# Value projection as seven block products, with context sums made in the load buffers

## The chip, the cores and the metric

The kernel runs on one core of one Trainium2 chip. Its time is the device time of one execution in microseconds (us), and the median of several executions is compared. Five engines work side by side, each through its own queue of instructions in order: TensorE (PE; the loading of its weights is shown apart as PEld), VectorE (DVE), ScalarE (ACT), GpSimd (POOL) and SyncE (SP, which here only issues transfers). Transfers between the chip's main memory and the on-chip memory run on 16 DMA engines.

## The reference

One layer of a perceiver: cross-attention of 64 queries to a context of 1024 rows for each of 16 batch items, then self-attention, then a quantised feed-forward part. The change touches the two projections of the context, `key @ Wk` and `value @ Wv`.

```python
def _L0_xattn_ref(query, key, value, Wq, Wk, Wv, Wo):   # key = value = ctx, 16 x 1024 x 1024
    q = (query @ Wq).reshape(b, sq, 32, 32).transpose(0, 2, 1, 3)
    k = (key @ Wk).reshape(b, sk, 8, 32).transpose(0, 2, 1, 3)      # Wk: 1024 x 256
    v = (value @ Wv).reshape(b, sk, 8, 32).transpose(0, 2, 1, 3)    # Wv: 1024 x 256
    k = jnp.repeat(k, 4, axis=1)
    v = jnp.repeat(v, 4, axis=1)
    scores = jnp.einsum('bhqd,bhkd->bhqk', q, k) * 32 ** -0.5
    probs = jax.nn.softmax(scores, axis=-1)
    out = jnp.einsum('bhqk,bhkd->bhqd', probs, v)
    return out.transpose(0, 2, 1, 3).reshape(b, sq, 1024) @ Wo

x = x + _L0_xattn_ref(_layernorm(x), ctx_4096, ctx_4096, Wq, Wk, Wv, Wo)
x = x + _L0_attn_ref(_layernorm(x), ...)
x = x + _L0_ffn_ref(_layernorm(x), ...)
```

All of this part is in 32-bit floats.

## The kernel before

The cross-attention is a loop over 32 units, n = 0 to 31. Unit n belongs to batch item b = n // 2 and to one half g of the eight key heads. Each unit has four slots, i = 0 to 3, and every engine's instructions stand in the order in which the loop writes them. In a slot of unit n TensorE computes scores of the unit that follows (`by_key`, L575, two tiles of 128 keys, into two pairs of PSUM banks that are used again in the next slot). ScalarE copies them to on-chip memory (L587) while VectorE keeps a running maximum (L591 in slot 0, L594 after it); the two take turns on the two pairs. After slot 3 `reduce` finds the maxima of the unit (L599 to L606), and `spread` sends them through main memory to all partitions. In slots 1 and 2 the current unit's exponentials are made, two per slot: VectorE subtracts the maxima (L618, 128 x 2048, both inputs in on-chip memory), ScalarE takes exp (L619), and GpSimd adds up the rows (`sums`, L625 for the first tile, L628 after it). TensorE's products with the values (L637), the sums over partitions (L647) and the quotients (L656, L661, L663, L666) follow in slots 2, 0 and 1.

Between these, TensorE takes steps from a list, `fillers`: the projection of the next batch item's context to keys and values. `fill(2)` stands early in a slot, a second `fill` late in it. The list of item b + 1 is made at the start of unit 2b and is used up by the end of unit 2b + 1. For items 2 to 15 (`fast`: 1 <= b < 15, that is n = 2 to 29) `project_fast` makes it.

There the keys are not computed as eight block products but as seven. The context of an item is seen as 2 x 2 blocks, quarter(b, h, i): h is the half of the 1024 rows, i the half of the 1024 features. The weights are 2 x 2 blocks too, i the half of the features and g the half of the 256 columns. The sums of context blocks are made by transfers: SP loads a quarter into a buffer, and GpSimd issues transfers that add further quarters to it in place. `chained` holds quarter(1,0) + quarter(1,1), then also + quarter(0,0), then also + quarter(0,1); `paired` holds quarter(1,0) + quarter(0,0). Sums of weight blocks are made once (`weight_sums`, L366 to L369). The seven products are called z5, p1, p2, z6, z7, z4 and p3; each is four matmul calls of 512 columns (L407), made in two steps of two calls, and each result is taken out of PSUM by ScalarE (a copy, L442) or VectorE (L445, L453, L458, L463), with one more operation on GpSimd (L446). p2 adds to the bank of p1, and p3 to that of z5. The values are computed plainly (L426): for each of eight tiles of 128 rows eight calls of 256 columns, in steps of four calls, copied by ScalarE (L434). A 32-bit matmul call is two weight loads and two matmul instructions in the trace.

The context itself is loaded in halves of 2 MB by SP (`load_context`) into two buffers that are used in turn (`stream`, at 64 and 80 KB of the arena), and the quarters of `chained` and `paired` (8 and 16 KB) are transferred again beside them. Three PSUM banks hold the projection's products. A tile of keys (`kT`) is read by the score matmuls: those of slots 2 and 3 of unit 2b + 1 read the second half of the rows of item b + 1, first half of the columns (k21), which z7 and z4 make.

In all units up to the end of the preparation of the feed-forward weights, `treat_piece` has ScalarE work on a piece of these weights in some slots (L522, L526, L530), with a load or a store on SP. In unit 8 `thresholds` reduces over them.

## Time and profile before

| | us |
|---|---|
| median of 3 runs | 1867.86 (1863.75 to 1868.98) |
| span of the profiled execution | 1863.3 |
| units 2 to 29, first score group of the first to the end of the last | 260.08 to 1261.90 |
| a pair of units in the middle (two score groups 0, 875.31 to 945.51) | 70.2 |

The page of the profile gives, for the whole execution, the granted clock of TensorE in 40 slices (tenths of full speed) and the busy shares of the other engines:

```
PE   8999999999899999999999999999999999899999
DVE  3011587777877887877887887877524257775554
ACT  1233656665566776776776776544101123664221
POOL 1000446655565576576566565566503424455520
PEclk9999999999999999999999999999999999899999
```

One slice is 46.6 us. The stage in question fills slices 6 to 27. Its costliest groups (line, engine, operation, output and input, count, busy us, mean ns of one, idle time before them and what ended it):

```
L628 POOL TENSOR_TENSOR arena<-arena 128x1024 f32<-128x1024 f32 x192 | 541.7, 2821 | 20.5 <-ACT arena L619 8.5
L426 PE MATMUL v<-arena 128*128 128x256 f32 x1792 | 405.2, 382 | 1.2 <-ACT arena L442 1.2
L618 DVE TENSOR_TENSOR arena<-arena 128x2048 f32<-128x2048 f32 x128 | 373.5, 2958 | 4.3 <-DMA arena<-tops 4.3
L407 PE MATMUL z<-arena 128*128 128x512 f32 x560 | 260.6, 608 | 11.3 <-ACT arena L442 5.3
L594 DVE TENSOR_TENSOR arena<-t,arena 128x512 f32<-128x512 f32 x384 | 258.9, 688 | 211.6 <-PE t L575 155.3
L587 ACT COPY arena<-t 128x1024 f32<-128x1024 f32 x256 | 254.8, 1009 | 209.1 <-PE t L575 118.0
```

Matmuls are pipelined, so the mean of one is longer than the distance between two.

### The profile page before, as it was taken

The numbers are of one execution on the slowest core, as the hardware profiler recorded it, in microseconds if no ns is written. First come the engines' busy times: TensorE is split into PE (matmuls) and PEld (weight loads), VectorE is DVE, ScalarE is ACT, GpSimd is POOL, SyncE is SP. The second block draws the span as 40 slices with busy tenths as digits, with TensorE's granted clock in tenths as the row PEclk, the third lists the DMA queues.
The fourth block names the chain that finished last, engine by engine and source line by source line (L and its number), as shares of the span: only waits on it lengthen the run. The fifth ranks groups of instructions, "written<-read, shape, count | busy, mean of one in ns | idle before, by whom it ended". The sixth has DMA issues, their size and how long they took to land.

```text
span 1863.3 us, 26374 instructions
## 1 busy us (share of the span) xinstructions
PE 1822.5 (98%) x10880; PEld 1080.9 (58%) x10880; DVE 1219.1 (65%) x1436; ACT 926.5 (50%) x988; POOL 885.8 (48%) x505
## 2 busy tenths in 40 slices
PE   8999999999899999999999999999999999899999
PEld 5445565565565665665665665664446454566654
DVE  3011587777877887887887887877524257775554
ACT  1233656665566776776776776544101123664221
POOL 1000446655565576576566566565503424455520
PEclk9999999999999999999999999999999999899999
DMA  9234578777687787886787787663120032243201
GB/s 346 69 106 139 187 223 271 224 231 237 188 262 196 253 254 191 263 254 195 254 252 201 251 254 202 198 186 153 36 75 19 1 77 62 51 130 109 75 29 51
DMA packets 64264, 314.65 MB, mean 169 GB/s; under 512 B 10192, under 2 KB 19344, under 8 KB 47376
## 3 DMA queue, kind: packets, MB, share of 16 engines
q1 hardware_dynamic: 52848, 242.99, 37.1%
q0 software_dynamic: 10144, 67.88, 17.2%
q10 hardware_dynamic: 1152, 2.10, 0.3%
q8 instruction: 85, 1.39, 0.3%
q14 instruction: 35, 0.29, 0.0%
HBM read 293.74 MB, written 19.20 MB: 168 GB/s over the span
## 4 chain that ended last, share of the span: by engine, by line
PE 66%; DVE 2%; POOL 2%; ACT 1%; DMA 1%; issue 1%; ACTq 0%; POOLq 0%; DVEq 0%
PE v L426 15%; PE z L407 10%; PE wo L250 6%; PE t L575 5%; PE q L250 5%; PE o L637 5%; PE d L1040 4%; PE p L407 4%; PE g L961 3%; PE gu L961 3%; PE v L740 1%; PE k L250 1%; POOL arena L628 1%; DMA arena<-in_ctxT 1%; PE o L647 1%
## 5 line engine op out<-in xcount | busy, mean ns | idle before, releaser
L628 POOL TENSOR_TENSOR arena<-arena 128x1024 f32<-128x1024 f32 x192 | 541.7, 2821 | 20.5 <-ACT arena L619 8.5
L426 PE MATMUL v<-arena 128*128 128x256 f32 x1792 | 405.2, 382 | 1.2 <-ACT arena L442 1.2
L594 DVE TENSOR_TENSOR arena<-t,arena 128x512 f32<-128x512 f32 x384 | 258.9, 688 | 211.6 <-PE t L575 155.3
L426 PEld LDWEIGHTS v<-arena 128*128 128x128 f32 x1792 | 336.8, 190 | 78.6 <-issue 29.5
L618 DVE TENSOR_TENSOR arena<-arena 128x2048 f32<-128x2048 f32 x128 | 373.5, 2958 | 4.3 <-DMA arena<-tops 4.3
L587 ACT COPY arena<-t 128x1024 f32<-128x1024 f32 x256 | 254.8, 1009 | 209.1 <-PE t L575 118.0
L619 ACT ACTIVATE arena<-arena 128x2048 f32<-128x2048 f32 x128 | 244.6, 1911 | 168.6 <-DVE arena L618 167.8
L625 POOL TENSOR_TENSOR arena<-arena 128x1024 f32<-128x1024 f32 x32 | 75.8, 2368 | 524.6 <-ACT arena L619 491.1
L407 PE MATMUL z<-arena 128*128 128x512 f32 x560 | 260.6, 608 | 11.3 <-ACT arena L442 5.3
L250 PE MATMUL q<-arena 128*128 128x512 f32 x512 | 224.6, 595 | 0.6 <-ACT arena L287 0.6
L407 PEld LDWEIGHTS z<-arena 128*128 128x128 f32 x560 | 103.2, 192 | 138.1 <-issue 117.5
L250 PEld LDWEIGHTS q<-arena 128*128 128x128 f32 x512 | 95.6, 190 | 116.4 <-issue 114.3
L575 PE MATMUL t<-arena 32*128 32x256 f32 x2048 | 146.6, 400 | 1.3 <-ACT arena L346 1.2
L961 PEld LDWEIGHTS <-arena 128*128 128x128 bf16 x1024 | 98.8, 98 | 64.7 <-issue 13.7
L591 DVE TENSOR_REDUCE arena<-t 128x512 f32<-128x1024 f32 x64 | 74.7, 1204 | 90.9 <-PE t L575 90.9
L575 PEld LDWEIGHTS t<-arena 32*128 32x128 f32 x2048 | 93.1, 184 | 66.6 <-issue 61.4
L637 PE MATMUL o<-arena 128*32 128x256 f32 x2048 | 123.8, 382 | 0.0
L250 PE MATMUL wo<-arena 128*128 128x512 f32 x256 | 112.3, 595 | 0.3 <-ACT arena L287 0.3
L407 PE MATMUL p<-arena 128*128 128x512 f32 x224 | 108.2, 605 | 0.0
L637 PEld LDWEIGHTS o<-arena 128*32 128x32 f32 x2048 | 60.0, 109 | 68.7 <-issue 32.0
L722 POOL TENSOR_TENSOR arena<-arena 128x512 f32<-128x512 f32 x20 | 33.5, 1673 | 133.6 <-DVE arena L720 133.6
L961 PE MATMUL gu<-arena 128*128 128x344 fp8e4 x544 | 85.3, 314 | 9.6 <-ACT arena L969 6.5
(146 smaller groups left out, 1974.6 us busy)
## 6 DMA issues: line engine op xcount, KB each, us to landing
arena<-in_ctxT SPq DMA_DIRECT2D x31, 2048.0 KB, 11.4
arena<-in_ctxT POOLq DMA_DIRECT2D x56, 1024.0 KB, 11.4
arena<-in_ctxT SPq DMA_DIRECT2D x28, 1024.0 KB, 12.1
arena<-tops SPq DMA_DIRECT2D x48, 512.0 KB, 4.9
arena<-in_wg SPq DMA_DIRECT2D x32, 688.0 KB, 4.5
arena<-in_wu SPq DMA_DIRECT2D x32, 688.0 KB, 6.2
arena<-in_wd SPq DMA_DIRECT2D x32, 688.0 KB, 9.2
arena<-ternary POOLq DMA_DIRECT2D x26, 344.0 KB, 3.8
```

What stands on the lines that cost most here:

```text
L250: nc.tensor.matmul(made[0], lhsT=lhsT(k), rhs=rhs(k), start=(k == 0), stop=(k == KC - 1))
L407: nc.tensor.matmul(held[n], lhsT=weights[:, k, :], rhs=what()[:, k, :], start=(first and k == 0), stop=(k == 3), skip_group_check=not first,)
L426: nc.tensor.matmul(held[n][:, bass.ts(at, KVD)], lhsT=ctx_halves[b, h][:, k, bass.ts(kts[at], P)], rhs=wkvs[:, k, KVD:], start=(k == 0), s ...
L575: nc.tensor.matmul(ws[jj // 2][:, jj % 2, a, :], lhsT=self.kT[rows, self.g, bass.ts(i * 2 + a, P)], rhs=two_tiles[self.b // 2 % 2][rows, s ...
L587: nc.scalar.copy(pt[:, 2 * mine : 2 * mine + 2], ws[mine])
L594: nc.vector.tensor_tensor(m, w[:, :, a], m, ALU.max)
L618: nc.vector.tensor_tensor(pt, pt, by.to_broadcast([P, 4, 2, 256]), ALU.subtract)
L619: nc.scalar.activation(pt, pt, AF.Exp)
L625: nc.gpsimd.tensor_tensor(acc, pt[:, :, 0], pt[:, :, 1], ALU.add)
L628: nc.gpsimd.tensor_tensor(acc, acc, pt[:, :, a], ALU.add)
L637: nc.tensor.matmul(self.po[bass.ts(jj, HD), 0:256], lhsT=self.v[:, kt, bass.ts(self.g * 4 + jj, HD)], rhs=self.pts[i][:, jj, a, :], start= ...
L961: nc.tensor.matmul(ps[:, :CW], lhsT=xqT[t][:, k, :], rhs=wbs[n][i][:, k, :], start=(k == 0), stop=(k == KC - 1),)
```

## The change

The values of items 2 to 15 are now made of seven block products too. `product` has a `kind`: 0 for keys, as before, and 1 for values, where the context block is the stationary operand and the weight block (128 columns) the moving one: 16 calls of 128 columns for each product, in two steps of eight. The list of steps goes from 30 to 28, and the second `fill` of slot 2 takes one step instead of two. Both kinds read the same four buffers: the chain, `paired`, `second_in` and `last_in`. The context is no longer loaded in halves: p1 reads `paired` while it still holds one quarter, before the other is added to it, and p2 and z4 read quarters of their own. There are two chain buffers, used in turn by items, at 64 and 8 KB; `second_in` and `last_in` lie at 72 and 80 KB, and the second set of weight sums at 88 KB, in the room of the two stream buffers. Each kind has its results taken out by three ScalarE copies, four VectorE operations and two GpSimd operations; p3 no longer adds to z5's bank, and GpSimd adds z5's block instead. The transfers and some sums stand elsewhere in the loop.

```diff
-    chained, paired = (place(kb, [4, 512]) for kb in (8, 16))
-    w_sums = place(24, [4, 4, P])
+    chains = [place(kb, [4, 512]) for kb in (64, 8)]
+    paired, second_in, last_in = (place(kb, [4, 512]) for kb in (16, 72, 80))
+    w_sums = [place(kb, [4, 4, P]) for kb in (24, 88)]
...
+    def load_quarter(dst, *of):
+        nc.sync.dma_start(dst, quarter(*of))
+
+    def add_quarter(dst, *of):
+        nc.gpsimd.dma_start(dst, quarter(*of), accum_op=ALU.add)
+
+    def chain_of(b):
+        return chains[b % 2]
...
+                else:
+                    for kt in (2 * i, 2 * i + 1):
+                        for k in range(4):
+                            nc.tensor.matmul(
+                                ps[:, bass.ts(kt, P)],
+                                lhsT=what[:, k, bass.ts(kt, P)],
+                                rhs=weights[:, k, :],
+                                start=(first and kt == 0 and k == 0),
+                                stop=(k == 3),
+                                skip_group_check=True,
+                            )
...
-        def after_z7(ps):
-            nc.vector.tensor_tensor(k21, ps, k12, ALU.subtract)
-            nc.gpsimd.tensor_tensor(k22, k21, k22, ALU.subtract)
...
+            def after_z6(ps, o12=o12):
+                nc.vector.tensor_tensor(o12, o12, ps, ALU.subtract)
+
+            def after_z7(ps, o12=o12, o21=o21, o22=o22):
+                nc.vector.tensor_tensor(o21, ps, o12, ALU.subtract)
+                nc.gpsimd.tensor_tensor(o12, o12, o22, ALU.add)
+                nc.gpsimd.tensor_tensor(o22, o21, o22, ALU.subtract)
+
+            def add(out):
+                return lambda ps: nc.vector.tensor_tensor(out, ps, out, ALU.add)
+
+            made.append(
+                {
+                    "z5": product("z5", kind, kind, s, chain, copy(o22)),
+                    "p1": product("p1", kind, (2, 0)[kind], b11, paired, copy(o12)),
+                    "p2": product("p2", kind, (2, 0)[kind], b21, second_in, copy(o11), first=False),
+                    "z6": product("z6", kind, (1, 2)[kind], t, chain, after_z6),
+                    "z7": product("z7", kind, (0, 2)[kind], w7, paired, after_z7),
+                    "z4": product("z4", kind, 1, w4, last_in, add(o21)),
+                    "p3": product("p3", kind, (0, 2)[kind], b22, chain, add(o12)),
+                }
+            )
-        steps = z5 + p1 + values(0, (0,), y_bank) + p2 + z6 + values(0, (1, 2), x_bank)
-        steps += z7 + p3 + z4 + values(0, (3,), y_bank)
-        steps += values(1, (0, 1), z_bank) + values(1, (2, 3), x_bank)
+        keys, values = made
+        steps = keys["z5"] + values["z5"] + keys["p1"] + values["p1"] + keys["p2"] + values["p2"]
+        steps += keys["z6"] + values["z6"] + keys["z7"] + keys["z4"] + values["z7"]
+        steps += keys["p3"] + values["z4"] + values["p3"]
...
-                if not odd and fast:
-                    if i == 2:
-                        load_context(b + 1, 1)
-                if odd and b + 2 < B:
-                    if i == 1:
-                        begin_chain(b + 2)
-                    if i == 2:
-                        load_context(b + 2, 0)
-                        begin_pair(b + 2)
+                if b + 2 < B and i == 1 - (n == 1) and n == max(2 * b, 1):
+                    load_quarter(chain_of(b), b + 2, 1, 0)
                 if n == 1 and i == 1:
-                    weight_sums()
+                    weight_sums(0)
+                if n == 2 and i == 0:
+                    weight_sums(1)
+                if n == 2 and i < 2:
+                    load_quarter((second_in, last_in)[i], 2, i, 1)
+                if odd and fast and b + 2 < B and i == 0:
+                    load_quarter(second_in, b + 2, 0, 1)
...
                 fill(2)
-                if i == 0 and not odd and fast:
-                    add_to_chain(b + 1, 0, 0)
+                if fast:
+                    if odd and i == 0:
+                        add_quarter(chain_of(b + 1), b + 1, 0, 1)
+                    if not odd and i == 1:
+                        add_quarter(chain_of(b + 1), b + 1, 0, 0)
+                    if not odd and i == 2:
+                        add_quarter(paired, b + 1, 1, 0)
+                        unit.sums(1)
...
-                if i == 1 and not odd and fast:
-                    add_to_pair(b + 1)
...
-                fill(1 if i == 0 and fast else 2)
+                if odd and i == 2 and b + 2 < B:
+                    load_quarter(paired, b + 2, 0, 0)
+                fill(1 if i in (0, 2) and fast else 2)
...
-                if i == 2 and held_back:
-                    add_to_chain(b + 1, 0, 1)
-                    unit.sums(1)
-                    unit.sums(2)
-                if i == 1 and odd and b + 2 < B:
-                    add_to_chain(b + 2, 1, 1)
+                if i == 1 + (n == 1) and odd and b + 2 < B:
+                    add_quarter(chain_of(b + 2), b + 2, 1, 1)
+                if i == 3 and odd and fast and b + 2 < B:
+                    load_quarter(last_in, b + 2, 1, 1)
```

At the end of the stage the loads of the output projection's weights and of the results stand up to two slots earlier or later (units 29 and 30).

## The prediction

> **What bounds the kernel now.** I read the busy table first, then the windows over two units in the middle.
>
> ```profile
> PE 1822.5 (98%) x10880; PEld 1080.9 (58%) x10880; DVE 1219.1 (65%) x1436; ACT 926.5 (50%) x988; POOL 885.8 (48%) x505
> ```
>
> ```profile
> 875.00:910.00 35.00, 35.00 (x236) 23.62 (x236) 27.96 (x29) 24.78 (x20) 23.39 (x11) 1.00 0.73 240
> 910.00:945.00 35.00, 35.00 (x223) 20.78 (x221) 29.56 (x30) 23.96 (x22) 20.78 (x12) 1.00 0.81 224
> ```
>
> TensorE has no gap here, but VectorE is busy 28 to 29.6 us of 35, far above its 65% over the span. So I followed VectorE in time through one odd unit, n = 19, from its second score group (L575) to the first of the next unit, with TensorE, ScalarE and GpSimd beside it.
>
> ```profile
> 884.02 1.15 PE L575 MATMUL t<-arena 32*128 32x256 f32 x16
> ...
> 910.45 1.15 PE L575 MATMUL t<-arena 32*128 32x256 f32 x16
> ```
>
> ```profile
> 885.26 2.74 DVE L594 TENSOR_TENSOR arena<-t,arena 128x512 f32<-128x512 f32 x4 [2.73 <-PE t L575]
> 888.91 0.69 DVE L463 TENSOR_TENSOR arena<-z,arena 128x512 f32<-128x512 f32 x1 [0.91 <-PE z L407]
> 889.51 4.48 DVE L618 TENSOR_TENSOR arena<-arena 128x2048 f32<-128x2048 f32 x2
> 893.92 1.75 DVE L656 RECIPROCAL arena<-o 128x256 f32<-128x256 f32 x1
> 895.70 0.42 DVE L663 TENSOR_TENSOR arena<-o,arena 128x256 f32<-128x256 f32 x1
> 896.04 2.73 DVE L594 TENSOR_TENSOR arena<-t,arena 128x512 f32<-128x512 f32 x4
> 898.69 7.32 DVE L618 TENSOR_TENSOR arena<-arena 128x2048 f32<-128x2048 f32 x2
> 905.93 1.40 DVE L594 TENSOR_TENSOR arena<-t,arena 128x512 f32<-128x512 f32 x2
> 908.88 1.42 DVE L594 TENSOR_TENSOR arena<-t,arena 128x512 f32<-128x512 f32 x2 [1.55 <-ACT arena L587]
> ```
>
> ```profile
> 896.79 7.06 POOL L628 TENSOR_TENSOR arena<-arena 128x1024 f32<-128x1024 f32 x2
> 903.79 2.47 POOL L666 COPY arena<-arena 128x256 f32<-128x256 f32 x1
> ```
>
> ```profile
> 906.04 1.91 ACT L619 ACTIVATE arena<-arena 128x2048 f32<-128x2048 f32 x1 [2.00 <-DVE arena L618]
> 907.86 1.91 ACT L587 COPY arena<-t 128x1024 f32<-128x1024 f32 x2
> ```
>
> Three things are to be seen. The score banks are single: the group at 910.45 needs the maxima that VectorE ends at 908.88 + 1.42 = 910.30, so in the odd unit VectorE is level with TensorE already, 0.15 us ahead of it. The last maxima wait for a ScalarE copy that stands behind the last exponential, so they end about 4.4 us after the last subtraction L618 (906.01 to 910.30). And L618 takes 2.24 us beside an idle GpSimd (4.48 for two at 889.51) but 7.32 for two beside its sums, which are stretched too (7.06 for two; the first sum of the unit, with VectorE elsewhere, takes 2.37): the two take turns, and here it costs VectorE 2.9 us. In the even unit the maxima end at 943.86 and the next group starts at 945.51, a slack of 1.65.
>
> **Parts of the change. TensorE.** Per context tile (one batch item's 1024 rows) the keys keep their 28 calls of 512 columns, 56 instructions. The values go from 64 calls of 256 columns to 112 of 128; each f32 call is two loads and two matmuls, so 128 pairs become 224.
>
> ```profile
> 38.79 0.80 PEld L285 LDWEIGHTS n1p<-ident,arena 128*128 128x128 f32 x7 [0.29 <-issue]
> 39.55 0.30 PEld L250 LDWEIGHTS k<-arena 128*128 128x128 f32 x2
> ...
> 418.47 2.56 PEld L426 LDWEIGHTS v<-arena 128*128 128x128 f32 x12 [0.24 <-issue]
> ```
>
> At 256 columns a pair takes (2.56 - 0.19) / 11 = 0.2155 us. The transposes, 128 columns, are spaced (0.80 - 0.14) / 6 = 0.110. Their loads are short (mean 0.141, against 0.190 of an f32 product), but the L250 load at 39.55 is a full one issued under the last 128-column transpose, and the load after it follows 0.30 - 0.19 = 0.11 later. So a full load just fits behind 128 columns. I take 0.111, with bounds 0.109 (the tightest spacing) and 0.190 (a load's whole duration, nothing hidden). Values: 128 x 0.2155 = 27.6 before, 224 x 0.111 = 24.9 after (24.4 to 42.6): 2.7 us less per tile. With three steps instead of four in slot 2, TensorE's own unit is 8.78 us for slot 0 and 24.9 for slots 1 to 3, 67.4 per tile.
>
> A rule speaks against this: the Trainium skill, "TensorE: Matmul & The Clock Gate", part 3 on row/col tiling, the mechanism, says that a weight load overlaps matmuls in flight only where the row group differs. In this trace the loads of L426 lie inside the matmul before them, in the same rows, or a pair could not take 0.2155. If load and product took turns, at 0.107 (128 columns at 1.2 GHz, its figure) + 0.109, the 224 pairs would take 48 us, and the tile about 21 us more than before.
>
> **Evacuations.** ScalarE's copies go from eight to six per tile, 0.3 to 0.6 us each, now two or more products ahead of the bank's next use; that removes most of the z6 stalls of the early tiles (TensorE idle 1.1 to 1.7 us before L407 at 281, 354, 374 and 428 us). VectorE gets four more 512-column operations per tile, GpSimd three more:
>
> ```profile
> L446 POOL TENSOR_TENSOR arena<-arena 128x512 f32<-128x512 f32 x14 | 18.0, 1283 | 0.2 <-DVE arena L445 0.2
> ```
>
> The built order of the changed kernel puts seven of VectorE's eight into the odd unit, where there is no slack. Inside the chain shown above it goes: z7 of the keys before the first L618, z4 of the keys between the first two, z7 of the values before the third, p3 of the keys between the last two. And z4's add waits for GpSimd, whose L446 still reads the block that it overwrites. Before, GpSimd did this in slot 0, far ahead.
>
> The walk, in us from the second score group of an odd unit: maxima end 3.97 (row); z7 of the keys 4.6 (0.65 each, L463 less its overlap); first L618 to 6.8 (2.2); GpSimd's two operations take their turn after it, 2 x 1.29, to 9.4; z4's add 10.1. The third score group reads this block, so it starts at 10.25 instead of 8.26. GpSimd's first sum (2.37) runs 9.4 to 11.75, since the exponential was ready at 8.8; the second L618 waits for it, 13.95. Reciprocal and product 16.1; maxima 18.75; z7 of the values 19.4. GpSimd's second sums run 16.0 to 20.75, so the third L618 ends at 22.95; p3 23.55; GpSimd's value operation goes first, to 24.25; the last L618 26.45; plus 4.4 and 0.1: 30.95. TensorE would need 24.9 and waits 6 us, 2 before the third group and 4 before the next unit. Bounds: with only z4's wait left of the turns (less 1.65, 1.35 and 0.7) 27.25; with three full sums of 2.36 in the way 34.3.
>
> The even unit: maxima 3.97, two L618 to 8.3, reciprocal to 10.4, maxima to 13.07 as before. The paired add is issued at 11.3 (p1 of the values done), the sums run from 11.9, and the third and fourth L618 each wait for one: 16.45 and 21.0, so the next group comes at 25.5 (24.9, TensorE's, to 26.9).
>
> **DMA.** SP issues 4 MB of plain loads per tile instead of 6, GpSimd four adds as before, which it reaches in time: the add before p3 is issued some 5 us into the odd unit behind the last even sum, p3 reads it at 8.78 + 10.25 + 2.9 = 21.9, and an add takes 11.4 (median to landing). Nothing comes off the path for the lighter traffic: TensorE waited only 2.7 us for context between 200 and 1340 us. If that cover went, it would be up to 3 us per tile (14.7 to landing, the longest in the chain of waits).
>
> **Sum.** A tile: 8.78 + 30.95 + 8.78 + 25.5 = 74.0. The 14 tiles ran from 260.08 to 1261.90, 1001.8 us; 14 x 74.0 = 1036, or +34. Add 5 of the 8.5 us that unit 8 loses now to the threshold (a stall of 5.3 us and 6.8 us at a granted clock near 0.5), and 2 for the second set of weight sums (4 x 0.69 ahead of the first z5 of the values): +41. The profiled execution's span is 1863.3; 1904. The runs' median, 1867.9, lies 4.6 above that span: 1909.
>
> **The clock.** The 5.3 us stall brought a half clock, 4.8 us after TensorE went idle; stalls of 1.7 us and less brought none. Mine of 4 us ends before 4.8, so I take 0; the upper bound is 3.4 us per tile. The same page, part 1, gives an idle window of 3.4 us that runs free. By it about one in five of such stalls would be caught, some 9 us in all.
>
> **Rivals.** (1) Faster: GpSimd and VectorE miss each other. It decides if the odd chain stays below 29.2 (71.56 per tile is even). For it: the turns depend on the start of each sum. Against: z4's wait alone is 2.6. At the low bounds, 17.6 + 27.25 + 24.9 = 69.7 per tile, 26 us less: 1842. (2) No change: the turns cost what they cost before besides z4's wait, and the early stalls go: about 1868. (3) Weight loads show: 224 x 0.190 - 128 x 0.2155 = 15 us per tile on TensorE, over VectorE's chain: 14 x (70.2 + 15) is 191 over the stage, 2059. The load at 39.55 speaks against it. That the change doesn't do what it says is excluded by the built order.
>
> **Chances.** Forecast 0.70 (own range 1885 to 1950), rival 1 0.20, rival 2 0.06, rival 3 0.04. About 0.3% (5.6 us) can be told from no change. Faster 0.20, same 0.06, slower 0.74. The range 1848 to 1948 leaves out the best end of rival 1, rival 3, and the case of three full turns.
>
> **What would show it.** Right: score groups in odd units 2 us late at the third and some 4 us late at the unit's end, TensorE waiting there for VectorE; L618 slowed in slot 1 too; value pairs spaced 0.109 to 0.112. Wrong: odd units of 33 to 34 us with TensorE without a gap, or pairs at 0.19.

## The result, and the profile after

| | before | after |
|---|---|---|
| median of the runs on the same chip, us | 1865.8 (1862.85 to 1868.98) | 1937.34 (1935.62 to 1938.36) |
| span of the profiled execution, us | 1863.3 | 1933.8 |
| mean granted clock of TensorE | 0.995 | 0.974 |
| units 2 to 29, us | 1001.8 | 1068.7 |
| a pair of units, mean of eight in the middle, us | 70.2 | 75.1 (odd 39.0, even 36.0) |
| the first pair of the stage, us | 72.7 | 84.4 |

The changed kernel takes 1.038 times as long (95% interval 1.037 to 1.040). It was predicted at 1909 in a range of 1848 to 1948. Of the 70.5 us between the spans 66.9 lie in units 2 to 29 and about 5.5 just behind them; unit 2 starts 1.8 us earlier.

First the busy table of the changed kernel, then its windows over an odd unit and the even unit behind it (columns: start:end, length, busy time of PE, PEld, DVE, ACT, POOL with counts, granted clock, DMA share, GB/s).

```profile
PE 1819.8 (94%) x12224; PEld 1122.3 (58%) x12224; DVE 1269.0 (66%) x1496; ACT 913.1 (47%) x960; POOL 988.8 (51%) x547
```

```profile
686.90:727.00 40.10, 34.05 (x288) 24.02 (x288) 30.96 (x33) 23.72 (x18) 26.73 (x13) 0.98 0.67 198
727.00:764.30 37.30, 36.31 (x264) 23.05 (x264) 29.88 (x30) 24.07 (x22) 24.69 (x11) 0.93 0.66 175
```

TensorE had no gap in such a pair before. Now it idles 6 us of the odd unit, and in the even unit its work takes longer, at a clock of 0.93. It isn't short of speed for the narrower products, as its weight loads in that unit show:

```profile
702.22 1.75 PEld L416 LDWEIGHTS z<-arena 128*128 128x128 f32 x15 [0.24 <-issue]
```

(1.75 - 0.19) / 14 = 0.111 us a pair, the value that was taken. So the time is lost in waits. The four engines in time, in the odd unit of the windows above (n = 13; the line numbers are those of the changed kernel: L573 the scores, L592 the maxima, L616 the subtractions, L617 exp, L585 the score copies; the columns are start and length in us, engine, line, operation, output and input, count, and in brackets the idle time before it and what ended it). VectorE:

```profile
697.12 2.74 DVE L592 TENSOR_TENSOR arena<-t,arena 128x512 f32<-128x512 f32 x4 [2.98 <-PE t L573]
699.78 0.68 DVE L444 TENSOR_TENSOR arena<-z,arena 128x512 f32<-128x512 f32 x1
700.38 2.28 DVE L616 TENSOR_TENSOR arena<-arena 128x2048 f32<-128x2048 f32 x1
705.16 0.69 DVE L449 TENSOR_TENSOR arena<-z,arena 128x512 f32<-128x512 f32 x1 [2.50 <-POOL arena L446]
705.77 2.28 DVE L616 TENSOR_TENSOR arena<-arena 128x2048 f32<-128x2048 f32 x1
...
710.10 1.40 DVE L592 TENSOR_TENSOR arena<-t,arena 128x512 f32<-128x512 f32 x2
713.20 1.42 DVE L592 TENSOR_TENSOR arena<-t,arena 128x512 f32<-128x512 f32 x2 [1.70 <-ACT arena L585]
...
725.56 1.42 DVE L592 TENSOR_TENSOR arena<-t,arena 128x512 f32<-128x512 f32 x2 [1.55 <-ACT arena L585]
```

TensorE's score groups:

```profile
706.00 1.15 PE L573 MATMUL t<-arena 32*128 32x256 f32 x16 [1.84 <-DVE arena L449]
...
727.13 2.09 PE L573 MATMUL t<-arena 32*128 32x256 f32 x16 [3.88 <-DVE arena L592]
```

ScalarE, and behind it the issues of SyncE and one of GpSimd:

```profile
699.54 1.54 ACT L524 ACTIVATE arena<-arena,magic,inverse 128x1376 f32<-128x1376 f32 x1
707.23 1.44 ACT L528 ACTIVATE arena<-arena,magic 128x1376 fp8e4<-128x1376 f32 x1 [6.15 <-DMA ternary<-arena]
708.57 3.69 ACT L617 ACTIVATE arena<-arena 128x2048 f32<-128x2048 f32 x2
712.17 1.90 ACT L585 COPY arena<-t 128x1024 f32<-128x1024 f32 x2
```

```profile
692.49 0.39 SPq L1156 DMA_DIRECT2D arena<-spilled  x1
692.98 0.39 SPq L379 DMA_DIRECT2D arena<-in_ctxT  x1
696.40 0.32 SPq L529 DMA_DIRECT2D ternary<-arena  x1
```

```profile
692.24 0.88 POOL L382 DMA_DIRECT2D arena<-in_ctxT  x1
```

Two causes are to be seen side by side. The third score group starts at 706.00 because the fourth product's add (L449) waited 2.50 us for GpSimd, as predicted. The other is not in the prediction at all: the changed kernel loads `second_in` in slot 0 of the odd units (L379, 1 MB), ahead of the store of a weight piece (L529) on SP. The store landed 10.7 us after its issue (median of all such stores 4.2), its buffer is single, and ScalarE's next piece (L528) waited 6.15 us for it. Everything behind it on ScalarE came late: both exponentials, then the score copies, for which the maxima waited at 713.20.

Two more things bear on this store. Every second odd unit (n = 13, shown, 17, 21, 25) has a load of 512 KB (L1156) ahead of it as well; these units take 39.8 to 40.1 us, the others 37.9 to 38.3. And the add of quarter (0,1), which the change has moved to this slot, is issued by GpSimd at 692.24 and runs beside the store. In the kernel before, which has neither this 1 MB load nor an add ahead of it in the slot, the first store of the odd units landed after 2.0 us (median of n = 9 to 27; 1.9 to 3.4), in the changed kernel after 9.7 (8.6 to 13.1). Other stores of this kind landed as late in the kernel before (median of all 7.1), but no engine waited for them.

The sum of these waits over ten tiles, from the list of waits (engine, line, what it waited for; us in total, times, longest):

```profile
ACT arena L528 <- DMA ternary<-arena: 46.2, 9, 6.2
...
DVE arena L592 <- ACT arena L585: 40.0, 26, 1.7
PE t L573 <- DVE arena L592: 33.5, 22, 3.9
...
DVE arena L449 <- POOL arena L446: 22.5, 9, 2.5
```

Of these the kernel before has only the second, at 24.1 us. The first tile has a wait of its own, here TensorE and then GpSimd:

```profile
258.33 1.15 PE L573 MATMUL t<-arena 32*128 32x256 f32 x16 [0.33 <-DVE arena L592]
266.61 6.14 PE L405 MATMUL z<-arena 128*128 128x512 f32 x8 [7.13 <-DMA arena<-in_ctxT]
```

```profile
244.80 13.70 POOL L626 TENSOR_TENSOR arena<-arena 128x1024 f32<-128x1024 f32 x4
258.43 1.07 POOL L382 DMA_DIRECT2D arena<-in_ctxT  x1
```

The add of quarter (1,1), moved to slot 2 in unit 1, is issued behind four sums, at 258.43, just when its first reader would start.

### The profile page after: what moved, and what is told of

The parts are those of the page before. It is cut to its first block, busy times and chain, and to the rows that moved or that the text cites. A ratio compares the mean times of both kernels' runs of the same rounds, so it can differ in the third digit from the quotient of the medians.

```text
span 1933.8 us, 29147 instructions
## 1 busy us (share of the span) xinstructions
PE 1819.8 (94%) x12224; PEld 1122.3 (58%) x12224; DVE 1269.0 (66%) x1496; ACT 913.1 (47%) x960; POOL 988.8 (51%) x547
## 4 chain that ended last, share of the span: by engine, by line
PE 51%; DVE 31%; ACT 6%; DMA 6%; issue 3%; POOL 2%; ACTq 0%; POOLq 0%; DVEq 0%
DVE arena L616 15%; PE q L251 10%; DVE arena L592 10%; PE wo L251 6%; PE z L405 4%; PE d L1038 4%; PE k L251 4%; PE t L573 3%; PE g L959 3%; PE gu L959 3%; DMA ternary<-arena 3%; PE o L635 3%; PE z L416 2%; PE v L340 2%; ACT arena L585 2%
## 5 line engine op out<-in xcount | busy, mean ns | idle before, releaser
L626 POOL TENSOR_TENSOR arena<-arena 128x1024 f32<-128x1024 f32 x192 | 547.8, 2853 | 24.2 <-ACT arena L617 12.7
L592 DVE TENSOR_TENSOR arena<-t,arena 128x512 f32<-128x512 f32 x384 | 259.6, 688 | 237.1 <-PE t L573 167.6
L616 DVE TENSOR_TENSOR arena<-arena 128x2048 f32<-128x2048 f32 x128 | 390.9, 3075 | 5.9 <-DMA arena<-tops 5.9
L585 ACT COPY arena<-t 128x1024 f32<-128x1024 f32 x256 | 254.1, 1009 | 230.9 <-PE t L573 106.9
L617 ACT ACTIVATE arena<-arena 128x2048 f32<-128x2048 f32 x128 | 243.0, 1908 | 183.2 <-DVE arena L616 183.2
L416 PEld LDWEIGHTS z<-arena 128*128 128x128 f32 x1792 | 216.8, 198 | 34.1 <-issue 31.5
L573 PE MATMUL t<-arena 32*128 32x256 f32 x2048 | 158.6, 426 | 74.9 <-DVE arena L592 47.9
L405 PE MATMUL z<-arena 128*128 128x512 f32 x448 | 220.1, 637 | 9.4 <-DMA arena<-in_ctxT 9.4
L416 PE MATMUL z<-arena 128*128 128x128 f32 x1792 | 227.6, 284 | 0.0
L573 PEld LDWEIGHTS t<-arena 32*128 32x128 f32 x2048 | 101.5, 195 | 127.1 <-issue 51.2
L416 PEld LDWEIGHTS p<-arena 128*128 128x128 f32 x1344 | 155.5, 192 | 16.0 <-issue 16.0
L251 PEld LDWEIGHTS q<-arena 128*128 128x128 f32 x512 | 95.6, 190 | 116.4 <-issue 114.3
L416 PE MATMUL p<-arena 128*128 128x128 f32 x1344 | 162.0, 277 | 0.0
L405 PEld LDWEIGHTS z<-arena 128*128 128x128 f32 x448 | 86.8, 204 | 111.1 <-issue 108.7
L405 PE MATMUL p<-arena 128*128 128x512 f32 x336 | 151.1, 592 | 0.0
L445 POOL TENSOR_TENSOR arena<-arena 128x512 f32<-128x512 f32 x28 | 75.6, 2699 | 101.1 <-DVE arena L444 101.1
## 6 DMA issues: line engine op xcount, KB each, us to landing
arena<-in_ctxT POOLq DMA_DIRECT2D x56, 1024.0 KB, 10.4
```

Of the source, the lines that this page charges most:

```text
L251: nc.tensor.matmul(made[0], lhsT=lhsT(k), rhs=rhs(k), start=(k == 0), stop=(k == KC - 1))
L405: nc.tensor.matmul(ps, lhsT=weights[:, k, :], rhs=what[:, k, :], start=(first and k == 0), stop=(k == 3), skip_group_check=not first,)
L416: nc.tensor.matmul(ps[:, bass.ts(kt, P)], lhsT=what[:, k, bass.ts(kt, P)], rhs=weights[:, k, :], start=(first and kt == 0 and k == 0), sto ...
L573: nc.tensor.matmul(ws[jj // 2][:, jj % 2, a, :], lhsT=self.kT[rows, self.g, bass.ts(i * 2 + a, P)], rhs=two_tiles[self.b // 2 % 2][rows, s ...
L585: nc.scalar.copy(pt[:, 2 * mine : 2 * mine + 2], ws[mine])
L592: nc.vector.tensor_tensor(m, w[:, :, a], m, ALU.max)
```

## The experiments

Times are medians beside runs of the kernel before on the same chip (1863.7 us with runs 1 to 4, 1865.6 to 1866.2 with the others). Pair, odd and even are means over eight tiles in the middle. Lines in kernels with added code are shifted by one or two.

### 1 and 2: GpSimd's two operations left out

```diff
-                nc.gpsimd.tensor_tensor(o12, o12, o22, ALU.add)
-                nc.gpsimd.tensor_tensor(o22, o21, o22, ALU.subtract)
+                if kind != 0:      # run 2: kind != 1
+                    nc.gpsimd.tensor_tensor(o12, o12, o22, ALU.add)
+                    nc.gpsimd.tensor_tensor(o22, o21, o22, ALU.subtract)
```

> Leaves out the two GpSimd operations behind z7 of the keys (two blocks of the keys are then wrong). My theory: VectorE's chain in the odd unit sets the time, and z4's add stands 2.5 us in it waiting for these two. Without them the third score group of an odd unit comes 8.3 us after the second (10.1 now), the chain ends near 28.6 us instead of 31.1, a tile takes about 2.6 us less, in all some 36 us less than the changed kernel's 1937: about 1900, 1890 to 1910. Rival: the four added VectorE operations by themselves make the unit long; then no more than 5 us go. Rival: TensorE's 128-column pairs; then nothing changes.

> Leaves out the two GpSimd operations behind z7 of the values (two blocks of the values are then wrong). My theory: nothing on VectorE waits for them directly, they only take turns with the last subtraction of the odd unit (about 1.3 us in some units): 10 to 20 us less, about 1923, 1912 to 1935. If the cost were GpSimd's load as such, this would save as much as leaving out those of the keys.

Measured: 1947.2 us (ratio 1.044, 1.041 to 1.047) without the keys' operations, 1939.2 (1.041, 1.038 to 1.044) without the values'. Neither gained anything; run 1 is even some 10 us slower than the changed kernel, its even units taking 37.0 us instead of 36.0; the cause of that is open. In run 1 the third score group did come 8.21 us behind the second instead of 10.11, but the unit ended no earlier. ScalarE and then VectorE in an odd unit of run 1:

```profile
712.15 1.44 ACT L529 ACTIVATE arena<-arena,magic 128x1376 fp8e4<-128x1376 f32 x1 [5.93 <-DMA ternary<-arena]
```

```profile
712.65 1.41 DVE L593 TENSOR_TENSOR arena<-t,arena 128x512 f32<-128x512 f32 x2
718.12 1.42 DVE L593 TENSOR_TENSOR arena<-t,arena 128x512 f32<-128x512 f32 x2 [4.06 <-ACT arena L586]
```

VectorE arrives at the third group's maxima earlier and waits 4.06 us there instead of 1.70: the score copy stands behind ScalarE's wait for the store. This wait was behind the one removed, and it pointed to the load.

### 3: TensorE kept busy through the stalls

```diff
-                    for kt in (2 * i, 2 * i + 1):
+                    again = {"z7": 2, "p3": 3}.get(name, 1) if i == 0 else 1
+                    for kt in (2 * i, 2 * i + 1) * again:
```

> Computes the same, but the first half of z7 of the values is multiplied twice and the first half of p3 of the values three times, 1.8 and 3.6 us of further TensorE work per tile, put where TensorE waits in the odd unit (2 us before the third score group, 4 us before the next unit). My theory: VectorE's chain sets the time and the low clock that follows these waits is the part of the loss that I left out; with the waits filled the granted clock stays at 1.0 in units 4 to 28 and the time falls although TensorE works 75 us more: 1905 to 1922. If the clock costs nothing there: 1937. If TensorE is the bound: 1990 or more.

Measured: 1927.7 us (1.034, 1.032 to 1.036), 9.6 less than the changed kernel but not in the expected 1905 to 1922, with 48 pairs (5.3 us at 0.111) more for TensorE in each tile. The clock went from 0.974 to 0.994, the even units from 36.0 to 34.7, the odd ones from 39.0 to 39.7. So the half clock behind the odd unit's stall cost 1.3 us in each even unit, some 18 us over the stage; the fill gave 0.6 a tile of that back.

### 4: the score group behind the first steps of a slot

```diff
+                behind = following and 1 <= b < B - 1 and i == (0, 2)[n % 2]
-                if following:
+                if following and not behind:
                     following.by_key(i)
...
                 fill(2)
+                if behind:
+                    following.by_key(i)
```

> Computes the same; in slot 0 of even units and slot 2 of odd units the score group stands behind the first two projection steps instead of ahead of them, so TensorE has 3.5 us of its own work where it waits for VectorE. My theory: VectorE's chain keeps its length, the clock stays at 1.0 and slot 0 of the even unit gets about 1.3 us shorter: some 3 us less per tile, about 1890, 1875 to 1910. If the order of VectorE's work alone counted and the clock did not, 1920. If it is GpSimd that is late: 1937.

Measured: 1938.8 us (1.040, 1.038 to 1.042), where 1875 to 1910 was expected. The group in slot 2 comes 1.8 us later and the one behind it 1.2 us earlier; the odd unit stays at 39.2, the pair at 75.1. Hiding the wait behind TensorE's steps doesn't help while ScalarE and VectorE are as late as before.

### 5 and 6: the load behind the store

```diff
-                if odd and fast and b + 2 < B and i == 0:
-                    load_quarter(second_in, b + 2, 0, 1)
...
                 if i < 3 and (n < 8 or i % 2 == 0 and (n, i) != (8, 0) or odd and i == 1):
                     treat_piece()
+                if odd and fast and b + 2 < B and i == 0:
+                    load_quarter(second_in, b + 2, 0, 1)
```

> In slot 0 of the odd units the 1 MB quarter load is issued behind the store of the weight piece instead of ahead of it on SP's queue. Theory A (the store waits behind the load on SP's queue and ScalarE waits for the store): the wait of ScalarE's treatment of a piece for the ternary store, 46.2 us in a window of ten tiles in the changed kernel, goes to under 5 us; VectorE's wait behind the third score copy (1.55 to 1.70 us each) with it; the wait of the third score group for z4's add behind GpSimd stays, so only a part comes back: 1905 to 1930 us. Rival B (ScalarE's lateness is hidden behind GpSimd and VectorE): the wait goes and the time stays, 1934 to 1941 us. Rival C (the store is slow for the amount of traffic, not for its place): the wait stays at 30 us or more and the time is 1932 to 1941 us.

> As the run before with the load behind the store, and GpSimd's two operations behind the seventh product of the keys are left out, so that the keys of blocks (1,2) and (2,2) lack those sums and the output differs. Theory A (two parallel causes hold the odd unit: GpSimd's sums and the late treatment by ScalarE; taking away one alone leaves the other): both waits gone, the odd unit falls from 38 to 40 us to about 34 to 36, and the time to 1875 to 1905 us, clearly under both runs that took one away. Rival B (VectorE's own work is the bound and no wait matters): within 10 us of the changed kernel, 1925 to 1945 us.

Measured: 1909.7 us (1.024, 1.022 to 1.026) for the load's place alone, 27.7 us less than the changed kernel; 1903.9 (1.021, 1.018 to 1.024) with the keys' operations left out as well. SyncE and ScalarE of the first, in the same odd unit as above, n = 13:

```profile
682.90 0.38 SPq L1154 DMA_DIRECT2D arena<-spilled  x1
686.82 0.32 SPq L529 DMA_DIRECT2D ternary<-arena  x1
687.19 0.63 SPq L512 DMA_DIRECT2D arena<-in_wg  x1
687.87 0.59 SPq L379 DMA_DIRECT2D arena<-in_ctxT  x1
```

```profile
695.32 1.44 ACT L528 ACTIVATE arena<-arena,magic 128x1376 fp8e4<-128x1376 f32 x1 [3.82 <-DMA ternary<-arena]
696.67 3.75 ACT L617 ACTIVATE arena<-arena 128x2048 f32<-128x2048 f32 x2
```

The exponential starts 10.4 us behind the second score group (686.31 there) instead of 12.7, no maxima wait for a copy in slot 2, and the odd unit ends 28.9 us after that group instead of 31.25. In the other kind of odd unit the exponential starts 8.9 us behind that group instead of 10.7. Units of the kind shown fall from 40.0 to 37.8 us, the others from 38.1 to 37.5. The wait for the store is down to 26.8 us in ten tiles, not under 5: the first store of the odd units still landed 7.0 us after its issue (median; 6.3 to 8.7). What held it then is seen in run 11. The time is inside theory A's range. GpSimd's wait, worth nothing while ScalarE was late (run 1), is worth 5.7 us now, less than A expected and hardly more than the two intervals tell apart.

### 7 and 8: the keys' steps earlier

```diff
-                fill(1 if i in (0, 2) and fast else 2)
+                fill(1 if (i == 0 or i == 2 and odd) and fast else 2)
...
+                behind = following and 1 <= b < B - 1 and i == 0 and n % 2 == 0     # run 8 alone
-                if i == 1 + (n == 1) and odd and b + 2 < B:
+                if i == 1 and odd and b + 2 < B:                                    # run 8 alone
                     add_quarter(chain_of(b + 2), b + 2, 1, 1)
```

Both have the load behind the store; `behind` is used as in run 4.

> The load behind the store, and slot 2 of the even units takes two steps, so that every later step of the keys, the seventh product with GpSimd's two operations among them, comes one step earlier: GpSimd has them done before the fourth product's add wants them. Nothing is left out. Theory A: z4's wait for GpSimd (32.5 us in thirteen waits in ten tiles of the changed kernel) and ScalarE's for the store are gone: 1880 to 1910 us. Rival B (the wait moves on to another slot, since VectorE's chain of 28 us is the bound of the odd unit): 1915 to 1940 us.

> As the run before, and the first tile's add of block (2,1) stands a slot earlier (slot 1 of unit 1), ahead of two of the four sums of GpSimd that it stood behind, and in slot 0 of the even units the next score group is formed behind the first step. Nothing is left out. Theory A: the first tile's wait of 7.1 us with the half clock behind it is gone, worth 7 to 10 us more than the run before: 1870 to 1900 us, still not under the kernel before, whose VectorE has about 4 us less to do in each tile. Rival B: the first tile's stall only moves, within 3 us of the run before.

Measured: 1950.3 us (1.047, 1.043 to 1.050) and 1935.9 (1.038, 1.035 to 1.041), far above theory A, and 40.7 us above run 5 for one step moved. GpSimd's wait was gone, the third group came 8.28 us behind the second, and yet the odd unit took 38.5 and its last slot up to 14 us. The end of such a unit, on VectorE, GpSimd and TensorE:

```profile
716.66 9.69 DVE L616 TENSOR_TENSOR arena<-arena 128x2048 f32<-128x2048 f32 x2
726.27 1.41 DVE L592 TENSOR_TENSOR arena<-t,arena 128x512 f32<-128x512 f32 x2
```

```profile
717.15 16.27 POOL L626 TENSOR_TENSOR arena<-arena 128x1024 f32<-128x1024 f32 x5
```

```profile
730.78 2.09 PE L573 MATMUL t<-arena 32*128 32x256 f32 x16 [7.36 <-DVE arena L592]
```

With no product's add between them the last two subtractions stand together, beside GpSimd's sums, and take 4.84 us each instead of the 3.18 and 3.86 of the changed kernel; the maxima stand behind both, and the next unit's score group waits 7.36 us. What decides the odd unit is what stands ahead of its last maxima. In run 8 the stage's first pair takes 72.5 us (the unit ahead of it 4.4 more), against 85.0 in run 7: some 8 us of the first tile's stall are the add's place.

### 9 and 10: the fourth product later, and the maxima first

```diff
-        steps += keys["z6"] + values["z6"] + keys["z7"] + keys["z4"] + values["z7"]
+        steps += keys["z6"] + values["z6"] + keys["z7"] + values["z7"] + keys["z4"]
...
                     following.by_key(i)
+                    if i == 3 and odd and fast:          # run 10
+                        unit.exponentials(3)
+                        unit.sums(3)
                     if i == 3:
                         following.reduce()
...
-                if i in (1, 2) and following:
+                if i in (1, 2) and following and not (i == 2 and odd and fast):     # run 10
                     unit.exponentials(2 * i - 1)
```

Both have the load behind the store and the first tile's add in slot 1. In both the score group of slot 2 now stands ahead of the last step of the fourth product, so it reads the keys' block (2,1) without that product and doesn't wait for it; the expectations do not say so.

> The load behind the store as in the earlier run of that edit (1909.7 us), and two more moves with nothing left out: the seventh product of the values is made ahead of the fourth product of the keys, so that GpSimd has one step more (about 2 us of products) before the fourth product's add wants its two sums; and the first tile's add of block (2,1) stands in slot 1 of unit 1 instead of slot 2. Theory A (VectorE's wait for GpSimd, 25.1 us in ten waits in a window of ten tiles, and the first tile's wait are each on the path): the third score group of the odd units comes about 8.4 instead of 10.1 us after the second, the odd unit falls from 37.5 to about 36 us, the first pair of units loses 7 to 10 us: 1878 to 1895 us. Rival B (VectorE's chain of some 27 us from slot 1 to the end of slot 3 is the bound, so that the wait only moves to slot 3): the odd units stay within 0.5 us of 37.5, only the first tile gains: 1899 to 1904 us.

> As the run before, and in the odd units the last subtraction, exponential and sums stand behind the maxima of the fourth score group instead of ahead of them; nothing is left out. The next unit's first score group waits only for those maxima, and the subtraction of 3.86 us stands ahead of them now. Theory A (VectorE's order at the end of the odd unit sets its length): 3 to 4 us off that wait, of which the next unit's second score group, which waits for its own maxima behind the subtraction and the reduction, gives back 0 to 2: 1 to 3 us a tile, 14 to 45 us: 1845 to 1880 us. Rival B (VectorE's total is the bound, and what is late at the end of the odd unit is late in slot 0 or 1 of the next): within 6 us of the run before.

Measured: 1889.6 us (1.012, 1.010 to 1.015) and 1878.0 (1.007, 1.005 to 1.009). From run 5 to run 9 the stage's first unit falls from 44.9 to 36.9 us (the add), the pair from 73.0 to 71.9. The maxima first take the odd unit from 36.6 to 34.1, and part of it comes back in the even unit, 35.3 to 36.7. VectorE and TensorE at the end of an odd unit of run 10:

```profile
762.64 1.40 DVE L592 TENSOR_TENSOR arena<-t,arena 128x512 f32<-128x512 f32 x2
765.00 1.42 DVE L592 TENSOR_TENSOR arena<-t,arena 128x512 f32<-128x512 f32 x2 [0.95 <-ACT arena L585]
766.33 2.62 DVE L616 TENSOR_TENSOR arena<-arena 128x2048 f32<-128x2048 f32 x1
```

```profile
768.83 1.15 PE L573 MATMUL t<-arena 32*128 32x256 f32 x16
...
778.90 0.64 PE L645 MATMUL o<-arena,ones 128*32 128x256 f32 x8 [1.56 <-POOL arena L626]
```

The next unit's group at 768.83 waits for nothing, but GpSimd's last sums are late, and the sums over partitions (L645) wait 1.56 us for them.

### 11: all in time by another order of the products

```diff
-        steps += keys["z6"] + values["z6"] + keys["z7"] + keys["z4"] + values["z7"]
-        steps += keys["p3"] + values["z4"] + values["p3"]
+        steps += keys["z6"] + keys["z7"] + values["z6"] + keys["z4"] + values["z7"]
+        steps += values["z4"] + keys["p3"] + values["p3"]
...
-                    if odd and i == 0:
+                    if odd and i == 1:
                         add_quarter(chain_of(b + 1), b + 1, 0, 1)
...
                 fill(2)
+                if i == 1 and fast and not odd:
+                    last.finish()
```

The load, the first add and the maxima stand as in run 10; `finish` leaves slot 0 of the even units.

> Nothing is left out. The seventh product of the keys stands ahead of the sixth of the values, so that GpSimd has its two sums done before the fourth product's add, which keeps its place; the add of block (0,1) to the chain follows the sixth product to slot 1, and the third product of the keys stands behind the fourth of the values to give that add time; the load behind the store and the first tile's add in slot 1 as before; the maxima of the fourth score group ahead of the last subtraction in the odd units; and in the even units the division's weight products stand in slot 1 instead of slot 0, so that they don't wait for the sums that GpSimd ends later now (1.56 us in the run before). Theory A (waits, not VectorE's total, made the changed kernel slow): odd units of 33.8 to 34.7 us as in the run before, even units back at 34.7 to 35.0, a pair of 68.6 to 69.6 against 70.2 before the change, no clock stretches but one or two: 1842 to 1866 us, at or under the kernel before. Rival B (VectorE and GpSimd have no room, every move makes a new wait): a pair of 70.5 us or more, 1875 us or more.

Measured: 1986.4 us (1.064, 1.062 to 1.066), the slowest of all; the pair is 79.7. VectorE and TensorE at the end of an odd unit:

```profile
732.19 0.69 DVE L449 TENSOR_TENSOR arena<-z,arena 128x512 f32<-128x512 f32 x1 [4.82 <-POOL arena L446]
...
742.79 1.27 DVE L449 TENSOR_TENSOR arena<-p,arena 128x512 f32<-128x512 f32 x2
```

```profile
743.61 2.09 PE L573 MATMUL t<-arena 32*128 32x256 f32 x16 [8.29 <-DVE arena L449]
```

Two new waits: the values' z4, a slot earlier, meets GpSimd's sums of the values' z7, which stand behind 7 us of row sums; and p3 of the keys, a slot later, is added behind the whole reduction, where the next score group, which reads that block, needs it at once.

One thing did get better. The add of quarter (0,1), on GpSimd's queue, now comes behind the first store of the odd unit and not ahead of it:

```profile
710.78 0.32 SPq L529 DMA_DIRECT2D ternary<-arena  x1
```

```profile
713.63 0.88 POOL L382 DMA_DIRECT2D arena<-in_ctxT  x1 [2.39 <-PE z L416]
```

This store landed after 1.9 us (median; 1.9 to 4.7), as in the kernel before, and ScalarE's wait for it fell from 26.8 us in ten tiles (run 5) to 0.2. The unit's second store, now behind the add, took 8.2 us instead of 3.1. In runs 6 to 10 and 12, which have the load behind the store and the add ahead of it, the first store takes 6.8 to 7.3 us in the median. So the load's place held the store for 2.7 us, and the add beside it for most of the rest. Load and add moved with nothing else changed were not tried.

### 12: the keys' sums on VectorE

```diff
+            by = (nc.vector, nc.gpsimd)[kind]
...
-                nc.gpsimd.tensor_tensor(o12, o12, o22, ALU.add)
-                nc.gpsimd.tensor_tensor(o22, o21, o22, ALU.subtract)
+                by.tensor_tensor(o12, o12, o22, ALU.add)
+                by.tensor_tensor(o22, o21, o22, ALU.subtract)
```

The products stand in the changed kernel's order; the load, the first add, the maxima and `finish` as in run 11.

> Nothing is left out, and the products keep the changed kernel's order. The two sums behind the seventh product of the keys are made by VectorE instead of GpSimd (about 1.3 us more on VectorE at 0.65 us each, against a wait of 2.5 us for GpSimd); the load behind the store, the first tile's add in slot 1, the maxima of the fourth score group ahead of the last subtraction in the odd units, and the division's weight products in slot 1 of the even units. Theory A (the waits made the changed kernel slow, and without them TensorE sets the pace again with about 2 us less work in a tile): third score group 8.3 to 8.9 us behind the second, odd units of 33.8 to 34.8 us, even ones of 34.7 to 35.2, a pair of 68.6 to 70.0 against 70.2 before the change, clock 0.99 or more: 1842 to 1866 us. Rival B (VectorE, with 1.3 us more to do, is the bound itself): odd units of 36 us or more, a pair of 71 us or more, 1876 us or more.

Measured: 1866.7 us, ratio 1.000 (0.999 to 1.001). The time is just outside theory A's range. The odd unit is 34.6, as expected, but the even one is 35.7 and the pair 70.3, above what theory A allowed. The clock is 1.00 all through the stage. Its windows over an odd unit and the next even one:

```profile
658.80:693.40 34.60, 33.77 (x288) 23.96 (x288) 29.73 (x35) 21.81 (x17) 19.04 (x11) 1.00 0.72 216
693.40:729.80 36.40, 34.52 (x266) 21.58 (x265) 31.57 (x31) 25.54 (x23) 27.95 (x11) 1.00 0.68 192
```

TensorE's work in the pair is 68.3 us against 70.2 before the change, and the stage takes 995.2 us against 1001.8. But 6.5 of these 6.6 us lie in the first three pairs; the eight pairs in the middle gain nothing, 70.3 against 70.2. The end gives the rest back:

```profile
1262.06 9.64 PE L251 MATMUL wo<-arena 128*128 128x512 f32 x16 [4.84 <-DVE arena L451]
```

The first product of the output projection takes a bank that the last product's add leaves only behind the reduction; the stall brings a half clock, and the first slot of unit 30 takes 17.9 us, 10.4 before. So this version is level with the kernel before and no better. The maxima's new place was not tried in the kernel before.

## Why the prediction was right in its sign and 28 us short

**TensorE.** Right: pairs at 0.111 us; rival 3 is out. TensorE's own work does fall (68.3 us of 70.2 in run 12, 67.4 predicted), but neither the changed kernel nor the middle pairs of run 12 get shorter by it.

**The third score group.** Right: 10.11 us behind the second, 10.25 predicted, by VectorE's wait for GpSimd. What it is worth was not: by itself nothing (run 1), since a wait that was not foreseen lay behind it.

**The odd unit's end.** Predicted 30.95 us behind the second group, measured 31.25 in the unit shown and 29.1 to 29.4 in the other kind, but not for the reason given. The step that failed is "GpSimd's first sum (2.37) runs 9.4 to 11.75, since the exponential was ready at 8.8": it was ready at 14.6 (708.57 + 1.9 - 695.88), and the second subtraction met no sum and ended at 12.2 instead of 13.95. In place of that turn VectorE waited 1.70 us for a score copy, which put the end of the maxima at 18.7, where 18.75 was predicted: that agreement is luck. Both the late exponential and the late copy come from one store: the prediction counted the transfers by their bytes and left out that ScalarE waits for this one. A quarter load had come ahead of it on SP's queue and an add of GpSimd beside it. The load's place costs 27.7 us (run 5), the size of the whole miss, but the miss is made up otherwise: beyond the forecast are some 8 us in the first pair, 6 in the next two, 11 in the other eleven and 5.5 behind the stage. That run 5 lands on 1909.7 is partly chance, since it holds the first tile's and the end's losses, which the forecast lacks, and shorter units.

**The clock.** Mis-sized: taken as 0 with a bound of 3.4 a tile. It is 1.3 us a tile (run 3), since stalls of 4 us do bring a half clock. The prediction had the 4.8 us from one stall; in the unit shown the clock fell at 725.56, 2.3 us after TensorE went idle at 723.25.

**The even unit.** 34.28 predicted; 34.7 where the clock holds (run 3), 36.0 in the changed kernel. Its last two subtractions, beside GpSimd's sums, take 8.43 us (at 824.56) for 7.9 predicted. With the odd unit the pair is 75.1 instead of 74.0.

**Missed.** The first tile's add on GpSimd's queue, 8.0 us from run 5 to run 9 in its unit, where the add was moved by one slot (run 9 reorders products too; runs 7 and 8 give about the same). The prediction did not walk it. And 5.5 us behind the stage, where the output projection waits for the bank of the last product (2.23 us and a half clock in the changed kernel).

**Rival 1** wanted a short odd chain: run 12 has one (25.8 us behind the second group), and its stage is 6.6 us shorter than before, where the rival had 26, and hardly any of that in the steady pairs. Of the 71 us, then, the load's place holds 28 and the first add 8. How the rest divides between GpSimd's wait, the order of the maxima and the end is not settled one by one: run 9 changes the computation, and run 12 moves several things at once.

## What to carry to other kernels

When transfers move, list for each small store that an engine waits for what stands ahead of it in its queue, and what other queues carry beside it: one load ahead of one small store cost 28 of the 71 us here, and an add on another queue held the same store longer still. Where two waits lie side by side, taking away the one that ends first shows nothing (run 1), taking away the later one does (run 5); look at what the freed engine waits for next before giving up the theory. And what stands ahead of the operation that frees a bank sets the length of the unit: one subtraction moved behind the maxima gave 2.5 us in the odd unit (1.1 in the pair), while steps moved so that two subtractions stood together ahead of them cost 41 us over the whole kernel.

## What the hardware did that was not expected

**The half clock comes from less idle time than a whole window.** The records show the granted clock falling on a grid of 3.413 us. Here is TensorE's idle time in each such window of units 2 to 29, summed from the matmul records, for the changed kernel and runs 3, 5, 9, 10 and 12, leaving out windows that ran at half clock already. All 18 windows with 2.2 to 3.4 us were followed by a half clock, 7 of the 10 between 1.9 and 2.2, 18 of the 39 between 1.5 and 1.9, and none of the 1333 under 1.5. The ends of matmuls are modelled in the records, so these bounds are rough by 0.2 to 0.3 us. The Trainium skill ("TensorE: Matmul & The Clock Gate", part 1, what's actually happening) has the clock fall after at least one idle window of about 3.4 us; here half to two thirds of a window were enough, and the measurement decides. A whole stretch at half clock lasts 3.41 us or a multiple: 95.6 us in all in the changed kernel from unit 2 to the slot behind the stage, 6.8 before, and 6.8 in run 12, there behind the stage.

**A small store landed late beside large transfers of its own queue and of another.** The first store of the odd units, 172 KB on SP's queue, landed after 9.7 us in the median with a load of 1 MB ahead of it and GpSimd's add of 1 MB issued 4.2 us earlier, after 7.0 with the load behind it (run 5), and after 1.9 with the add behind it too (run 11). The Trainium skill ("DMA: Bandwidth & Descriptors", two DMAs through the same engine are not ordered) says that descriptors within one queue of one DMA engine start in order; the 2.7 us by the load's place agree with that. The add stands in another queue. Issuing the store on a queue other than SP's was not tried.

**Turns between VectorE and GpSimd are dear when they follow each other.** A subtraction of 128x2048 takes 2.28 us alone, and 4.84 in the mean of two in run 7 with GpSimd's sums beside them, and those sums took 3.25 each (16.27 for five) instead of 2.36.
